# A filter phase rebuilt around pairs of units: four row groups, the sum of squares on VectorE, and queues held to program order

## The chip, the cores and the metric

The kernel runs on one core of a Trainium2 chip. The metric is the device time of one execution in microseconds (us). Engines are named as in the profile: PE is the matmul engine and PEld its weight loads, DVE is VectorE, ACT is ScalarE, POOL is GpSimd, SP is the queue that issues most transfers. All data is 32-bit floating point.

## The reference

Two layers are computed on an image batch of shape (4, 512, 512, 16). The first is a group norm, then a two-dimensional convolution whose filter is given in the frequency domain as a ratio of two polynomials, for each of 16 x 16 pairs of input channel i and output channel j:

```python
a = jnp.pad(denumerator, ((0,0),(0,0),(1,0),(1,0)), constant_values=1.0)
b = jnp.pad(numerators, ((0,0),(0,0),(0,0),(1,0),(1,0)), constant_values=0.0)
h_truncated = irfft2(rfft2(b, s=(l1, l2)) / rfft2(a, s=(l1, l2)), s=(l1, l2))
H_full = h0 + rfft2(h_truncated, s=(2*l1, 2*l2))[0]
y = irfft2(einsum('...hwi,ijhw->...hwj', rfft2(x, s=(2*l1, 2*l2)), H_full))[..., :l1, :l2, :]
```

The second layer is another group norm and a 3 x 3 convolution with normalised patches and an arccosine. Both layers are added to their inputs. The change concerns only the quotient of the two polynomials, evaluated at 512 x 512 frequencies for every pair (i, j).

## The kernel before

The program has four phases, one after another: the filter (`filter_phase`), the forward transform of the image, the convolution in frequency space, and the inverse transform with the second layer. The change lies wholly in the filter phase, the first 5840 us.

The filter phase is a software pipeline over 1024 units of work. A unit is one output channel j, one half h of the second frequency axis, one input channel i, and one half kp of the first frequency axis; the loop nests them in that order, kp innermost. A unit's tiles hold 128 partitions by 512 numbers: two blocks k of 128 first-axis frequencies, a real and an imaginary part c, and 128 second-axis frequencies.

Step v of the loop does, in program order:

- the next piece of `rest`, the odd frequencies of an output channel that is already done (`odd`): two matmuls of 512 columns into `pt` (L417), and the copy of the piece before it to `ot`, on DVE and ACT in turn (L423, L425), stored by SP. These begin once 72 units are done, so units 0 to 71 have none;
- every 64 steps `weights`, the polynomials of the next output channel;
- `polynomials` of unit v (L329): denominator (n = 0) and numerator (n = 1) are each evaluated by matmuls with a contraction of only 18 rows. The operands sit at partitions 32 (i mod 4) and 32 ((i mod 4) xor 1), so the two use two of the four 32-row groups of the matmul array. Each of the two PSUM tiles of a unit fills one bank; the pool `ps_ab` has four. ACT copies both to SBUF (`ab`, L335) and squares the denominator (`sq`, L337);
- every eight steps `quad` (L313, L315), which prepares the first-axis factors of four input channels: eight matmuls into four 32-column groups;
- `square` of unit v-1: POOL adds the two squares (`dn`, L341);
- `terms` of unit v-2: POOL makes real and imaginary part of the numerator from the products (L355, L356);
- `product` of unit v-1: DVE multiplies (`m`, L347) and takes the reciprocal (L348), POOL makes the two crossed products (`x`, L350 and L351);
- `quotient` of unit v-2: DVE scales both parts (`sp`, L361, two instructions) and, for h = 0, puts one column from `z` in (L364);
- `taps` of unit v-3: four matmuls with the whole array (`pg`, L372) and two ACT copies into the stage tile `st` (L377). After 32 units the two stage tiles go out to DRAM (L383). The stage pool has three tiles.

Beside all this, `image_stats` makes the group-norm statistics of the image (L544 on DVE, its loads issued by ACT).

Each engine runs its own queue in a fixed order. That order is made when the program is built: a scheduler places instructions greedily, by the dependencies and by a table of estimated durations, so an instruction that the program names late can be queued early. The statistics show it: the program spreads them over 1024 units, and in the trace they are done after 965 us.

Of the kernel before, what the change touches and what calls it, by code (L numbers as in the profile page):

```python
# [40 lines left out]
F32 = mybir.dt.float32  # L41
AF = mybir.ActivationFunctionType
# [4 lines left out]
P = 128  # L47
N = 512
B = 4
C = 16  # L50
# [150 lines left out]
def bc(ap, axis, shape):  # L201
    return ap.unsqueeze(axis).to_broadcast(shape)

# [21 lines left out]
def filter_phase(tc, cst, h0, num, den, g_d, beside):  # L229
    nc = tc.nc  # L230
    with ExitStack() as ctx:
# [3 lines left out]
        ew = ctx.enter_context(tc.tile_pool(name="f_ew", bufs=2))  # L235
# [3 lines left out]
        ps_ab = ctx.enter_context(tc.tile_pool(name="f_psab", bufs=4, space=PSUM))  # L239
# [4 lines left out]
        e2 = load_const(nc, cp, cst, "e2").rearrange("p (s h n) -> p s h n", s=2, h=2)  # L244
# [5 lines left out]
        def weights(j):  # L250

            sa = wt.tile([18, C, 32], F32, name="sa")
            sb = wt.tile([18, C, 32], F32, name="sb")
            nc.gpsimd.dma_start(out=sa.rearrange("p i n -> p (i n)"), in_=cst["apad"])
            nc.gpsimd.memset(sb, 0.0)
            for t, src in ((sa, den), (sb, num)):
                for c in range(2):
                    nc.gpsimd.dma_start(  # L260
                        out=t[9 * c + 1 : 9 * c + 9, :, 9 * c + 1 : 9 * c + 9],
                        in_=src[:, j].rearrange("i p q -> p i q"),
                    )
            ha = sm.tile([18, C, 18], F32, name="ha")
            nc.gpsimd.tensor_mul(ha, sa[:, :, 0:18], bc(h0b[:, j :: C], 2, [18, C, 18]))
            nc.gpsimd.tensor_add(sb[:, :, 0:18], sb[:, :, 0:18], ha)


            v = sm.tile([18, 2, 4, C], F32, name="v")
            ev = sm.tile([18, 2, 2, C], F32, name="ev")  # L270
            od = sm.tile([18, 2, 2, C], F32, name="od")
            for n, t in enumerate((sa, sb)):
                for c in range(2):
                    q = 9 * c
                    nc.vector.reduce_sum(ev[:, c, n, :], t[:, :, q : q + 9 : 2], axis=AX.X)
                    nc.vector.reduce_sum(od[:, c, n, :], t[:, :, q + 1 : q + 9 : 2], axis=AX.X)
            nc.vector.tensor_add(v[:, :, 0::2, :], ev, od)
            nc.vector.tensor_sub(v[:, :, 1::2, :], ev, od)
            pz = ps_t.tile([P, 4, 2, 4, C], F32, name="pz", tag="t")
            for k in range(4):  # L280
                nc.tensor.matmul(
                    pz[:, k].rearrange("p c v i -> p (c v i)"),
                    e1[:, k * P : (k + 1) * P],
                    v.rearrange("p c v i -> p (c v i)"),
                    start=True,
                    stop=True,
                )
            zs = sm.tile([P, 4, 2, 4, C], F32, name="zs")
            nc.scalar.copy(zs, pz)
            hz = sm.tile([P, 4, 2, 2, C], F32, name="hz")  # L290

            def half(c, v):
                return zs[:, :, c, v : v + 2, :].rearrange("p k v i -> p k (v i)")

            divide(nc, sm, half(0, 0), half(1, 0), half(0, 2), half(1, 2),
                   hz[:, :, 0].rearrange("p k v i -> p k (v i)"),
                   hz[:, :, 1].rearrange("p k v i -> p k (v i)"), [P, 4, 2 * C], "zd")
            z = wt.tile([P, 4, 2, C], F32, name="z")
            nc.vector.tensor_add(z[:, :, 0, :], hz[:, :, 0, 0, :], hz[:, :, 1, 1, :])
            nc.vector.tensor_sub(z[:, :, 1, :], hz[:, :, 1, 0, :], hz[:, :, 0, 1, :])  # L300
            return sa, sb, z

        def quad(sa, sb, iq):

            us = []
            for n, s in enumerate((sa, sb)):
                pu = ps_t.tile([P, N], F32, name=f"pu{n}", tag="t")  # L310
                for i in range(4):
                    at = 32 * (i ^ n)
                    nc.tensor.matmul(pu[at : at + 32], s[:, 4 * iq + i], e1, start=True, stop=True)  # L313
                u = wt.tile([P, N], F32, name=f"u{n}")
                nc.scalar.copy(u, pu)  # L315
                us.append(u)
            return us

        def polynomials(w):

            pp = [ps_ab.tile([P, 2, 2, P], F32, name=f"pab{n}", tag="ab") for n in range(2)]
            for k in range(2):
                k1 = (2 * w["kp"] + k) * P
                for n in range(2):
                    at = 32 * (w["i"] % 4 ^ n)
                    q = slice(at, at + 18)
                    nc.tensor.matmul(  # L329
                        pp[n][:, k].rearrange("p c n -> p (c n)"),  # L330
                        w["us"][n][q, k1 : k1 + P], e2[q, n, w["h"], :], start=True, stop=True,
                    )
            w["ab"] = [ew.tile([P, 2, 2, P], F32, name=f"ab{n}") for n in range(2)]
            for n in range(2):
                nc.scalar.copy(w["ab"][n], pp[n])  # L335
            w["sq"] = ew.tile([P, 2, 2, P], F32, name="sq")
            nc.scalar.activation(w["sq"], w["ab"][0], AF.Square)  # L337

        def square(w):
            w["dn"] = ew.tile([P, 2, P], F32, name="dn")  # L340
            nc.gpsimd.tensor_add(w["dn"], w["sq"][:, :, 0], w["sq"][:, :, 1])  # L341

        def product(w):

            a, b = w["ab"]
            w["m"] = ew.tile([P, 2, 2, P], F32, name="m")
            nc.vector.tensor_mul(w["m"], b, a)  # L347
            nc.vector.reciprocal(w["dn"], w["dn"])  # L348
            w["x"] = ew.tile([P, 2, 2, P], F32, name="x", bufs=1)
            nc.gpsimd.tensor_mul(w["x"][:, :, 0], b[:, :, 0], a[:, :, 1])  # L350
            nc.gpsimd.tensor_mul(w["x"][:, :, 1], b[:, :, 1], a[:, :, 0])  # L351

        def terms(w):
            m, x = w["m"], w["x"]
            nc.gpsimd.tensor_add(m[:, :, 0], m[:, :, 0], m[:, :, 1])  # L355
            nc.gpsimd.tensor_sub(m[:, :, 1], x[:, :, 1], x[:, :, 0])  # L356

        def quotient(w):
            sp = w["sp"] = ew.tile([P, 2, 2, P], F32, name="sp")
            for c in range(2):  # L360
                nc.vector.tensor_mul(sp[:, :, c], w["m"][:, :, c], w["dn"])  # L361
            if w["h"] == 0:
                kp = w["kp"]
                nc.vector.tensor_copy(sp[:, :, :, 0], w["z"][:, 2 * kp : 2 * kp + 2, :, w["i"]])  # L364
# [67 lines left out]
        def odds():  # L432

            for j in range(C):
                while done[0] < 64 * (j + 1) + 8:
                    yield
                yield from odd(j)

        work = [dict(j=j, h=h, i=i, kp=kp)
                for j in range(C) for h in range(2) for i in range(C) for kp in range(2)]  # L440
        done = [0]
        rest = odds()
        polys = {0: weights(0)}
        us = quad(*polys[0][:2], 0)
        for v in range(len(work) + 3):
            next(rest)
            if v % 64 == 32 and v < len(work) - 64:
                polys[v // 64 + 1] = weights(v // 64 + 1)
            if v < len(work):
                w = work[v]  # L450
                if v % 8 == 0 and v:
                    us = ahead
                w["us"], w["z"] = us, polys[w["j"]][2]
                polynomials(w)
                if v % 8 == 4 and v + 4 < len(work):
                    g = (v + 4) // 8
                    ahead = quad(*polys[g // 8][:2], g % 4)
            first, second, third = (work[v - k] if 0 <= v - k < len(work) else None for k in (1, 2, 3))
            if first:
                square(first)  # L460
            if second:
                terms(second)
            if first:
                product(first)
            if second:
                quotient(second)
            if third:
                if third["i"] == 0 and third["kp"] == 0:
                    st = [stp.tile([P, N, C], F32, name=f"st{a}", tag="st") for a in range(2)]
                third["st"] = st  # L470
                taps(third)
                done[0] += 1
                third.clear()
            if v % 2:
                next(beside, None)
# [915 lines left out]
```

## Time and profile before

| | |
|---|---|
| median of three runs | 18878.0 us (18847.71 to 18889.9) |
| profiled execution | 18884.85 us, of which the span of the core is 18883.1 us |
| filter units with statistics beside them | 0 to 1000 us (162 units) |
| the other filter units | 1000 to 5660 us (862 units) |
| odd frequencies of the last output channel | 5660 to 5840 us |
| forward transform | 5840 to about 6920 us |
| convolution and the last phase | 6920 us to the end |

Busy time in the two stages of the filter, in us:

| stretch | PE | DVE | ACT | POOL | granted PE clock |
|---|---|---|---|---|---|
| 0 to 1000 us | 820.74 | 864.04 | 457.75 | 674.54 | 0.85 |
| 1000 to 5660 us | 4462.42 | 3524.26 | 2642.29 | 3602.86 | 0.95 |

How to read it: a row of the groups names the line, the engine, the operation, the tile written and the tiles read, the shape and the number of instructions; after the bar stand the time in which at least one of them ran, the mean duration of one in ns, and the idle time of the engine just before them with what ended it. A 32-bit matmul appears as two records, so one call in the code is two instructions in a row of the profile. Matmuls overlap, so a record lasts longer than the step from one to the next.

### The profile page before, as it was taken

Reading aid. Unit: us, or ns where it says so; the run is one execution under the profiler, and the core shown is the slowest. Engines: PE = TensorE matmul, PEld = TensorE weight load, DVE = VectorE, ACT = ScalarE, POOL = GpSimd, SP = SyncE. Lnnn points to the kernel's source line nnn. Section 1 sums busy time; section 2 is a strip of 40 time slices with the busy share of each in tenths; the row PEclk is TensorE's granted clock in tenths of the full one; section 3 lists DMA queues with packets and bytes.
Section 4 is the critical chain, followed back from the end, with each engine's and each line's share of the span. In section 5 each row is a group of like instructions: output and inputs, shape, how many; then the busy total and the mean of one; then the engine's idle time right before and its main releaser. Section 6 shows DMA issues by size and latency. Waiting matters only on the chain. (4 is left out here: it accounts for less than half of the span.)

```text
span 18883.1 us, 533095 instructions
## 1 busy us (share of the span) xinstructions
PE 17055.0 (90%) x224908; PEld 12368.5 (66%) x224908; DVE 11526.1 (61%) x24155; ACT 9724.0 (51%) x17871; POOL 11616.7 (62%) x12701
## 2 busy tenths in 40 slices
PE   7899999999998998988888888888898988988898
PEld 5455555555554457777777777777777776877777
DVE  8877777777773335555555555555555555246887
ACT  4455555555552235555555555555555554005788
POOL 7577777777771126666666666666666666026776
PEclk8899999999999999999999999999999999998999
DMA  3755555455547668888888888888888888696432
GB/s 101 207 153 141 144 150 150 134 152 152 147 140 230 187 199 321 325 319 320 322 323 318 324 318 320 322 323 321 323 322 320 324 324 306 248 326 208 161 127 71
DMA packets 2918838, 4543.16 MB, mean 241 GB/s; under 512 B 117634, under 2 KB 2086492, under 8 KB 2809566
## 3 DMA queue, kind: packets, MB, share of 16 engines
q1 hardware_dynamic: 2686254, 3768.92, 59.1%
q0 software_dynamic: 174896, 605.89, 8.3%
q10 hardware_dynamic: 55296, 134.24, 2.1%
q8 instruction: 1773, 29.05, 0.6%
q14 instruction: 619, 5.07, 0.1%
HBM read 3031.24 MB, written 1477.31 MB: 239 GB/s over the span
## 5 line engine op out<-in xcount | busy, mean ns | idle before, releaser
L783 PE MATMUL pg<-c_dg,g 64*128 64x128 f32 x32832 | 2855.2, 291 | 347.3 <-ACT gh L683 193.2
L799 PE MATMUL pm<-xe,gh 128*32 128x64 f32 x131328 | 2394.6, 222 | 555.4 <-issue 297.3
L799 PEld LDWEIGHTS pm<-xe,gh 128*32 128x32 f32 x131328 | 2011.6, 111 | 1153.2 <-issue 962.1
L783 PEld LDWEIGHTS pg<-c_dg,g 64*128 64x128 f32 x32832 | 2292.4, 190 | 695.3 <-issue 257.2
L372 PE MATMUL pg<-c_dinv,sp 128*128 128x256 f32 x8192 | 2279.4, 426 | 296.0 <-ACT st L377 179.1
L828 DVE TENSOR_TENSOR z<-zq,pz 128x256 f32<-128x256 f32 x2052 | 861.8, 420 | 2665.9 <-ACT zq L827 2591.7
L348 DVE RECIPROCAL dn<-dn 128x256 f32<-128x256 f32 x1024 | 1790.8, 1749 | 774.7 <-POOL dn L341 774.6
L372 PEld LDWEIGHTS pg<-c_dinv,sp 128*128 128x128 f32 x8192 | 1611.1, 207 | 944.3 <-issue 213.0
L681 DVE COPY gh<-pg 128x512 f32<-128x512 f32 x2046 | 1410.0, 689 | 1247.7 <-PE pg L783 1244.0
L417 PE MATMUL pt<-ev_in,c_todd 128*128 128x512 f32 x4096 | 1974.9, 607 | 51.9 <-DMA ev_in<-g_d 27.3
L752 POOL TENSOR_TENSOR xu<-xe,c_late 128x256 f32<-128x256 f32 x2052 | 1393.7, 705 | 893.1 <-ACT xe L683 866.3
L683 ACT COPY yf<-pm 128x512 f32<-128x512 f32 x2046 | 1210.9, 592 | 935.8 <-PE pm L799 921.5
L335 ACT COPY ab<-pab 128x512 f32<-128x512 f32 x2048 | 1103.9, 591 | 1126.3 <-POOL m L355 323.9
L377 ACT COPY st<-pg 128x256 f32<-128x256 f32 x2048 | 1072.6, 622 | 1025.4 <-PE pg L372 629.3
L763 ACT COPY xe<-xl 64x1024 f32<-64x1024 f32 x513 | 538.6, 1050 | 1891.4 <-POOL xl L754 1891.4
L350 POOL TENSOR_TENSOR x<-ab,ab 128x256 f32<-128x256 f32 x1024 | 874.7, 854 | 922.9 <-ACT ab L335 896.4
L683 ACT COPY gh<-pg 128x512 f32<-128x512 f32 x2058 | 1201.1, 584 | 392.3 <-PE pg L783 383.0
L820 PE MATMUL pz<-c_ident,yf 128*128 128x128 f32 x8208 | 1373.7, 290 | 29.8 <-issue 28.0
L417 PEld LDWEIGHTS pt<-ev_in,c_todd 128*128 128x128 f32 x4096 | 807.5, 198 | 680.0 <-issue 518.2
L329 PEld LDWEIGHTS pab<-c_e,u 18*128 18x128 f32 x8192 | 719.0, 187 | 806.1 <-ACT st L377 458.3
L754 POOL TENSOR_TENSOR xl<-xl,xu 128x1024 f32<-128x1024 f32 x513 | 1209.7, 2358 | 40.2
L329 PE MATMUL pab<-c_e,u 18*128 18x256 f32 x8192 | 1186.5, 406 | 5.6 <-ACT ab L335 5.6
(205 smaller groups left out, 33831.8 us busy)
## 6 DMA issues: line engine op xcount, KB each, us to landing
xe<-xf_d SPq DMA_DIRECT2D x1026, 1536.0 KB, 10.7
g<-g_d SPq DMA_DIRECT2D x511, 1024.0 KB, 9.9
g_d<-st SPq DMA_DIRECT2D x64, 4096.0 KB, 34.5
ev_in<-g_d SPq DMA_DIRECT2D x1024, 256.0 KB, 4.8
g_d<-ot SPq DMA_DIRECT2D x1024, 256.0 KB, 2.8
xf_d<-xe POOLq DMA_DIRECT2D x513, 448.0 KB, 8.4
xf_d<-xl POOLq DMA_DIRECT2D x513, 448.0 KB, 5.4
x_d<-xo SPq DMA_DIRECT2D x128, 1024.0 KB, 5.1
```

The source lines that it names most:

```text
L329: nc.tensor.matmul(pp[n][:, k].rearrange("p c n -> p (c n)"), w["us"][n][q, k1 : k1 + P], e2[q, n, w["h"], :], start=True, stop=True,)
L335: nc.scalar.copy(w["ab"][n], pp[n])
L348: nc.vector.reciprocal(w["dn"], w["dn"])
L372: nc.tensor.matmul(pg[:, k].rearrange("p a x -> p (a x)"), w["sp"][:, k, c, :], dinv[:, 2 * kp + k, c, :], start=(c == 0), stop=(c == 1),)
L417: nc.tensor.matmul(pt, todd[:, c, kc, hh * P : hh * P + P], ev[:, kc, c], start=(kc == 0), stop=(kc == 1),)
L681: nc.vector.tensor_copy(dst, src)
L683: nc.scalar.copy(dst, src)
L752: nc.gpsimd.tensor_mul(u[:, :, h, c], xe[:, :, h, 1 - c], bc(late[:, 1 + c], 2, [P, F, 2]))
L754: nc.gpsimd.tensor_add(xl.rearrange("p f h c k -> p (f h c k)"), xl.rearrange("p f h c k -> p (f h c k)"), u.rearrange("p f h c k -> p (f ...
L783: nc.tensor.matmul(pg[c][:, j % 4], g[half, j], dg[half], start=True, stop=True)
L799: nc.tensor.matmul(pm[32 * q : 32 * q + 32, g % 8], gh[:, f].rearrange("p c j -> p (c j)"), xe[:, :, f].rearrange("p t h c k -> p t (h c k ...
L820: nc.tensor.transpose(pz[:, t % 4].rearrange("p v q x -> p (v q x)"), y[:, at].rearrange("p g x -> p (g x)"), ident)
```

## The change

Units are now made in pairs that share kp, h and j and whose input channels differ by two: (0,2), (1,3), (4,6), (5,7) and so on.

- `polynomials` takes a pair. It issues the eight matmuls of both units together, and since i mod 4 differs by two, the four polynomials lie in four different row groups. The pair takes all four PSUM tiles at once.
- The eviction becomes a function of its own, still per unit. The copies stay; the one square of 512 numbers is split in two of 256. The square of the real part goes to SBUF, the square of the imaginary part goes back into the denominator's PSUM tile, which therefore stays in use until it is read.
- `square` moves from POOL to DVE, reads one square from SBUF and one from PSUM, and now belongs to unit v, at the end of step v. `dn` gets three buffers.
- The two crossed products on POOL become one instruction of 512 numbers, the two scalings on DVE become one with `dn` repeated over the two parts.
- `quad` moves behind the units' work of the step.
- The class `InOrder` ties every unit instruction of PE, DVE, ACT and POOL to the one before it on its engine, so that the scheduler keeps these in program order. The work of `rest`, `weights`, `quad` and the statistics is not tied.

```diff
+class InOrder:
+    def __exit__(self, *_):
+        dep = mybir.DependencyInfo(mybir.DependencyClass.NoSync, mybir.DependencyReason.DATA)
+        for i in list(self.tc.nc.cur_bb.bb.instructions)[self.begin :]:
+            if i.engine in self.engines:
+                if i.engine in self.last:
+                    self.tc.add_manual_dep(i, self.last[i.engine], dep, reason="in order")
+                self.last[i.engine] = i.name
...
-        def polynomials(w):
-            pp = [ps_ab.tile([P, 2, 2, P], F32, name=f"pab{n}", tag="ab") for n in range(2)]
+        def polynomials(pair):
+            for w in pair:
+                w["pp"] = [ps_ab.tile([P, 2, 2, P], F32, name=f"pab{n}", tag="ab") for n in range(2)]
             for k in range(2):
-                k1 = (2 * w["kp"] + k) * P
-                for n in range(2):
...
+                for w in pair:
+                    k1 = (2 * w["kp"] + k) * P
+                    for n in range(2):
+                        at = 32 * (w["i"] % 4 ^ n)
+                        q = slice(at, at + 18)
+                        nc.tensor.matmul(
+                            w["pp"][n][:, k].rearrange("p c n -> p (c n)"),
+                            w["us"][n][q, k1 : k1 + P], e2[q, n, w["h"], :], start=True, stop=True,
+                        )
+
+        def evict(w):
             w["ab"] = [ew.tile([P, 2, 2, P], F32, name=f"ab{n}") for n in range(2)]
+            pp = w.pop("pp")
             for n in range(2):
                 nc.scalar.copy(w["ab"][n], pp[n])
-            w["sq"] = ew.tile([P, 2, 2, P], F32, name="sq")
-            nc.scalar.activation(w["sq"], w["ab"][0], AF.Square)
+            w["sq"], w["pa"] = ew.tile([P, 2, P], F32, name="sq"), pp[0]
+            nc.scalar.activation(w["sq"], w["ab"][0][:, :, 0], AF.Square)
+            nc.scalar.activation(pp[0][:, :, 1], w["ab"][0][:, :, 1], AF.Square)
 
         def square(w):
-            w["dn"] = ew.tile([P, 2, P], F32, name="dn")
-            nc.gpsimd.tensor_add(w["dn"], w["sq"][:, :, 0], w["sq"][:, :, 1])
+            w["dn"] = ew.tile([P, 2, P], F32, name="dn", bufs=3)
+            nc.vector.tensor_add(w["dn"], w["sq"], w.pop("pa")[:, :, 1])
...
-            nc.gpsimd.tensor_mul(w["x"][:, :, 0], b[:, :, 0], a[:, :, 1])
-            nc.gpsimd.tensor_mul(w["x"][:, :, 1], b[:, :, 1], a[:, :, 0])
+            nc.gpsimd.tensor_mul(w["x"], b, a[:, :, ::-1])
...
-            for c in range(2):
-                nc.vector.tensor_mul(sp[:, :, c], w["m"][:, :, c], w["dn"])
+            nc.vector.tensor_mul(sp, w["m"], bc(w["dn"], 2, [P, 2, 2, P]))
...
+                with order:
+                    if v % 2 == 0:
+                        pair = work[v : v + 2]
+                        pair[1]["us"] = us
+                        polynomials(pair)
+                    evict(w)
+            with order:
+                if second:
+                    terms(second)
+                if first:
+                    product(first)
+                if second:
+                    quotient(second)
+                if v < len(work):
+                    square(w)
+            if v % 8 == 4 and v + 4 < len(work):
+                g = (v + 4) // 8
+                ahead = quad(*polys[g // 8][:2], g % 4)
             if third:
...
-                taps(third)
+                with order:
+                    taps(third)
```

## The prediction

> **What bounds the kernel now.** I read the busy shares by stretch first, then the order of time inside one stretch, then the groups of that stretch and its waits.
>
> ```profile
> 1000.00:5660.00 4660.00, 4462.42 (x19043) 2652.02 (x19042) 3524.26 (x4514) 2642.29 (x4965) 3602.86 (x4478) 0.95 0.53 147
> ```
>
> The columns after the length are PE, PEld, DVE, ACT, POOL, clock, DMA share, GB/s. PE is busy 96%, every other engine 57 to 77%. The groups of this stretch count 862 products, so a unit takes 4660 / 862 = 5.41 us. A busy PE need not be at its peak, so I looked at the order of time:
>
> ```profile
> 3002.15 1.13 PE L329 MATMUL pab<-c_e,u 18*128 18x256 f32 x8
> 3003.21 1.99 PE L372 MATMUL pg<-c_dinv,sp 128*128 128x256 f32 x8
> 3005.05 1.88 PE L417 MATMUL pt<-ev_in,c_todd 128*128 128x512 f32 x4
> 3006.86 1.13 PE L329 MATMUL pab<-c_e,u 18*128 18x256 f32 x8
> 3007.92 1.06 PE L313 MATMUL pu<-c_e,sa 18*32 18x512 f32 x8
> ...
> 3009.77 1.56 PE L372 MATMUL pg<-c_dinv,sp 128*128 128x256 f32 x6
> ```
>
> From start to start, PE spends 1.06 us on the polynomials of a unit, 1.84 on its taps, 1.81 on a piece of odd frequencies, and 1.85 on a quad every eighth unit, with no gap. That is 1.06 + 1.84 + 1.81 + 1.85/8 = 4.94 us per unit. So PE itself sets 4.94 of the 5.41 us, and 0.47 are stalls. The largest stall that I can name:
>
> ```profile
> ACT st L377 <- DMA g_d<-st: 202.6, 27, 9.7
> ```
>
> It is 27 waits of 7.5 us (0.24 us a unit): a new stage tile waits until the third-last one has gone out. The rest is the start of each output channel and refilling after these waits.
>
> ```profile
> L348 DVE RECIPROCAL dn<-dn 128x256 f32<-128x256 f32 x862 | 1508.8, 1750 | 716.7 <-POOL dn L341 716.7
> L347 DVE TENSOR_TENSOR m<-ab,ab 128x512 f32<-128x512 f32 x862 | 751.6, 872 | 323.5 <-ACT ab L335 300.6 <-ACT st L377 0.5 <-issue 0.2
> L361 DVE TENSOR_TENSOR sp<-m,dn 128x256 f32<-128x256 f32 x1727 | 921.2, 574 | 0.0
> ```
>
> DVE waits 0.83 us a unit for POOL's sum of squares, and is second in line. The product takes 0.69 us undisturbed (its median over the phase), 0.87 here; the two scalings 2 x 0.35 undisturbed, 2 x 0.53 by their busy time. So 0.5 to 0.55 us per unit goes to DVE standing behind POOL.
>
> The first 1000 us are different: 162 units at 6.0 us (966 us from the first reciprocal), DVE busy 864 us because all 283 us of statistics (1024 x 276 ns) fall there, and no odd piece in the first 72 units. There DVE is the bound.
>
> **What the skill says.** The Trainium skill, "TensorE: Matmul & The Clock Gate", section "Measured speedup vs the span model", gives 3.07x for four row tiles of 32 rows by 512 columns. No run of before has four row groups. The trace has two: the 8 records of a unit start in pairs 6 ns apart, 216 ns from pair to pair, while taps make one record per 216 ns. And it has four column groups (L313), whose records start in fours within 20 ns and 429 ns apart. "TensorEngine Tiling (Array Packing)", section "Key Properties", says that changing the tiling mode drains the array; the trace agrees: 4 x 216 = 864 of the 1062 ns are streaming, about 104 are the first weight load and 94 the drain. "SBUF — State Buffer", section "Who interferes with whom", says that a DVE instruction with two SBUF inputs contends with a POOL instruction that reads SBUF, and that one with a single SBUF input does not. The trace agrees: in the second pair of lines below DVE issued 0.03 us after POOL and took 1.24 us, not 0.69.
>
> ```profile
> 3001.41 0.68 DVE L347 TENSOR_TENSOR m<-ab,ab 128x512 f32<-128x512 f32 x1
> 3001.43 1.24 POOL L341 TENSOR_TENSOR dn<-sq 128x256 f32<-128x256 f32 x1
> ...
> 3006.16 0.72 POOL L341 TENSOR_TENSOR dn<-sq 128x256 f32<-128x256 f32 x1
> 3006.19 1.24 DVE L347 TENSOR_TENSOR m<-ab,ab 128x512 f32<-128x512 f32 x1
> ```
>
> **The change part by part** (per unit, stretch after 1000 us).
>
> *Pairs in four row groups.* If four groups stream together, a pair is 16 records in four rounds: 104 + 4 x 216 + 94 = 1062 ns, or 0.53 per unit, saving 0.53. Upper bound of the cost: the groups go two by two, 8 rounds less one mode change, about 0.96 per unit, saving 0.1. A loss I exclude, since the same records in the same groups do not get longer by standing in a row. I take 0.53: the quad's records pass three waiting ones to reach a free group, so PE's queue can feed four. PE is then 0.53 + 1.84 + 1.81 + 0.23 = 4.41 us per unit.
>
> *Sum of squares.* POOL loses an add of 0.92 (mean here). DVE gains one of 256 numbers with one input in PSUM; the nearest row, of the convolution phase, is
>
> ```profile
> L828 DVE TENSOR_TENSOR z<-zq,pz 128x256 f32<-128x256 f32 x2052 | 861.8, 420 | 2665.9 <-ACT zq L827 2591.7 <-POOL z L838 71.7
> ```
>
> so +0.42 on DVE, and its 0.83 us of waiting for POOL is gone. The split square costs ACT one fixed part more: 512 numbers take 591 ns from PSUM (L335) and 256 take 377 (L827), so 0.84 ns a number and 0.16 fixed; +0.16 at most. ACT was busy 3.07 us per unit (2642/862), so 3.2 after: hidden below PE and DVE as long as it isn't waited for at once. It is waited for at the pair's start, see the rivals.
>
> *Merged products.* POOL's two products (0.85 + 0.96) become one of 512: 1.27 by the row of L836 (1273 ns). POOL falls from 4.18 to about 2.9. DVE's two scalings become one like the product, 0.69.
>
> *DVE's sum:* reciprocal 1.75 + product 0.69 + scaling 0.69 + add 0.42 + column 0.37/2 + odd copy 0.68/2 = 4.07. Behind POOL it stood 0.5; POOL reads SBUF for less time but is packed closer, so I keep 0.45 (ends: 0.2, and 0.97, which is a whole crossed product of 1.27 issued just ahead of each scaling, less the 0.3 us for which the reciprocal still covers it). With the 0.1 us per unit of weights work on DVE (7 us per 64 units), 4.6 us.
>
> *Program order and quad's place.* No instruction costs more. The queues of before already ran pab, pg, pt in the program's order (lines above). A quad is used four steps later, so its later place is covered by four units of work; without cover it would cost 1.85/8 = 0.23 per unit, what PE pays anyway. SP's issues stay where they were, one step after their copies; POOL's own transfers belong to `weights` and aren't tied. The new wait is that a pair needs all four PSUM tiles back. Behind it on PE stand taps of v-3 and v-2 and two odd pieces; for these ACT's stage copies and the odd copies wait.
>
> *Sum.* The bound moves from PE (4.94) to DVE (4.6), PE following at 4.41. Stalls that nothing here touches: stage waits 0.24 and some 0.1 of refilling. So 4.6 + 0.34 = 4.94 against 5.41: -0.47 x 862 = -405. The loop by which PE waits for DVE and DVE for PE will not be perfect: I give 0.08 back, +70. In the first 162 units DVE is the bound already: +0.42 for the add, -0.12 for one fixed part less in the scaling, about -0.15 of standing behind POOL: +0.15 x 162 = +25. The tail of odd frequencies (180 us) and all later phases stay. Total -310: from the profiled 18884.85 to 18575, which against the median of the runs (18878.0, 7 us lower) I give as 18570.
>
> **Rivals.**
> 1. *PE stays the bound and DVE hides fully.* 4.41 + 0.34 = 4.75: -0.66 x 862 = -570, first stage 0: 18,310. For it: POOL loses nearly a third of its work. Against: DVE's 4.07 leaves only 0.34 for standing behind POOL and weights.
> 2. *The four groups don't run together* (the change doesn't do what it says). PE stays at 4.84, gain 0.1 x 862 = 86, less the 25 of the first stage, less a pair's longer turn-round: 18,850. Against it: the quad's four-way starts.
> 3. *Slower: the PSUM turn-round becomes the bound.* Before, two units' tiles could be filled while two were read; now nothing is filled until DVE's add of the pair's second unit has read the last square. The loop: pair 1.06, ACT's four steps of the first unit 1.85, add 0.42, product 0.69, reciprocal 1.75, scaling 0.69 with 0.97 behind POOL, add 0.42, four hand-overs of 0.1, odd copy 0.68, half a column 0.18: 9.1 us per pair, just under the 9.2 that DVE needs anyway. It decides from (5.41 - 0.34) x 2 = 10.1 us on. If PE is in the middle of a 1.8 us piece whenever the add ends, up to 1.8 us come on top; with 1.5, the loop is 10.6: (5.3 + 0.34 - 5.41) x 862 = +200, first stage +25: 19,100. Against it: PE's other work between two pairs is 7.3 us, so in a steady loop PE has nothing left and stands at the pair when the add ends.
>
> **How the numbers follow.** Forecast as summed (18,400 to 18,720): 0.55. Rival 1: 0.10. Rival 2 and a partial gain with much lost in the loop (18,720 to 18,840): 0.13, and 0.05 within 0.2% (38 us, about what a measurement of this kernel can tell from no change). Rival 3: 0.17. Faster 0.78, same 0.05, slower 0.17. The range 18,400 to 18,860 leaves out rival 1's lower part (0.07) and most of rival 3 (0.13).
>
> **What would show it.** The polynomials' records starting in fours, a pair taking 1.06 to 1.3 us from start to start (2.0 under rival 2); 862 units of the later stretch at 4.9 to 5.1 us; reciprocals no longer waiting for POOL; DVE busier than PE (88 to 95%). PE waiting ahead of a pair's first matmul for DVE's add, by more than 1 us a pair, would show rival 3. The prediction is wrong if the scaling stands behind POOL for the whole 1 us in every unit, if the statistics are queued elsewhere, or if ACT's order makes the second unit's eviction late behind a stage copy that waits for its transfer.

## The result and the profile after

The changed kernel takes 18389.05 us (median of three runs, 18373.56 to 18397.62) against 18878.0 us: a ratio of 0.9745 with a 95% interval of 0.9731 to 0.9759, or 489 us less. It is faster, as forecast. The saving is larger than the 310 us of the sum, and the time lies 11 us below the low end of the range.

Where the time went, from the two profiled executions (spans 18883.1 and 18387.3 us, so -496):

| part | before, us | after, us | difference |
|---|---|---|---|
| first three output channels (192 units), from reciprocal to reciprocal | 1128.4 | 1076.4 | -52 |
| the other 831 units | 5.408 each | 4.906 each | -417 |
| whole filter phase, up to the first forward transform | 5847.8 | 5377.8 | -470 |
| forward transform | 1090.8 | 1088.3 | -2 |
| convolution | 9053.6 | 9033.7 | -20 |
| what follows | 2890.9 | 2887.5 | -3 |

The code of the convolution is unchanged. Over the profiles of all kernels of this study that phase took between 9012.8 and 9085.6 us, so its -20 is put down to nothing here.

The first view is that of busy times by stretch, for the stretch that answers to the one shown of before. The columns are again PE, PEld, DVE, ACT, POOL, clock, DMA share, GB/s.

```profile
1000.00:5160.00 4160.00, 3923.64 (x18703) 2382.49 (x18702) 3490.54 (x4541) 2572.07 (x5718) 2569.60 (x2706) 0.95 0.58 162
```

It holds 846 units, 4.92 us each. PE is busy 94%, DVE 84%, and POOL has fallen from 77% to 62%. The order of time on PE, for one pair:

```profile
4263.02 1.15 PE L352 MATMUL pab<-c_e,u 18*128 18x256 f32 x16
4264.10 1.99 PE L398 MATMUL pg<-c_dinv,sp 128*128 128x256 f32 x8
4265.93 1.88 PE L443 MATMUL pt<-ev_in,c_todd 128*128 128x512 f32 x4
4267.65 1.89 PE L398 MATMUL pg<-c_dinv,sp 128*128 128x256 f32 x8
4269.37 1.88 PE L443 MATMUL pt<-ev_in,c_todd 128*128 128x512 f32 x4
4271.18 1.15 PE L352 MATMUL pab<-c_e,u 18*128 18x256 f32 x16
```

Sixteen records of polynomials, a whole pair, take 1.08 us from start to start, where eight took 1.06. In the trace they start in fours, 6 to 8 ns apart within a four; the fours follow each other by 0.32 us once and by 0.216 us twice. The pair takes 8.16 us, 4.08 a unit. DVE and POOL of the same kernel, one step before (start, duration; a bracket is idle time and what ended it):

```profile
4259.03 1.74 DVE L376 RECIPROCAL dn<-dn 128x256 f32<-128x256 f32 x1
4259.18 0.73 POOL L382 TENSOR_TENSOR m<-m 128x256 f32<-128x256 f32 x1 [0.63 <-DVE m L375]
4259.99 0.72 POOL L383 TENSOR_TENSOR m<-x 128x256 f32<-128x256 f32 x1
4260.69 0.62 DVE L387 TENSOR_TENSOR sp<-m,dn 128x512 f32<-128x512 f32 x1
4260.79 1.66 POOL L378 TENSOR_TENSOR x<-ab,ab 128x512 f32<-128x512 f32 x1
4261.83 0.40 DVE L369 TENSOR_TENSOR dn<-sq,pab 128x256 f32<-128x256 f32 x1
4262.16 0.83 DVE L375 TENSOR_TENSOR m<-ab,ab 128x512 f32<-128x512 f32 x1
4262.91 1.74 DVE L376 RECIPROCAL dn<-dn 128x256 f32<-128x256 f32 x1
```

The scaling (L387) issues 0.1 us ahead of the crossed product (L378) and takes its undisturbed 0.62 us. It is the crossed product that is longer: 1.66, where its shortest is 1.256. The product (L375) then stands behind the crossed product. Two groups and three waits of the stretch (groups: busy, mean ns, idle before and its releaser; waits: us in total, times, longest):

```profile
L376 DVE RECIPROCAL dn<-dn 128x256 f32<-128x256 f32 x846 | 1471.5, 1739 | 0.0
L369 DVE TENSOR_TENSOR dn<-sq,pab 128x256 f32<-128x256 f32 x845 | 347.5, 411 | 470.5 <-ACT pab L365 468.7
```

```profile
ACT st L403 <- DMA g_d<-st: 275.7, 26, 13.1
PEld pab L352 <- DVE dn L369: 82.6, 53, 3.6
PE pab L352 <- DVE dn L369: 59.7, 39, 3.2
```

The reciprocals wait for nobody. The add costs 0.41 us and waits 0.55 us a unit for ACT's second square. PE and its weight loads wait for DVE's add at most 142 us in 423 pairs. And the wait for the stage tile has grown: 26 waits of 10.6 us, where there were 27 of 7.5.

In the steps from one reciprocal to the next, after the first three channels, every 32 units (one h) hold one or two long steps, those that wait for the stage tile. Before: 13.2 and 7.0 us, the other thirty 5.10 on average. After: 18.1 us, the other thirty-one 4.48. So 5.10 + 0.31 became 4.48 + 0.43 us a unit, the second term being what the long steps have over the others, shared out over 32.

### The profile page after: what moved, and what is told of

It reads as the page before. It is cut to its first block, busy times and chain, and to the rows that moved or that the text cites. A ratio compares the mean times of both kernels' runs of the same rounds, so it can differ in the third digit from the quotient of the medians.

```text
span 18387.3 us, 530668 instructions
## 1 busy us (share of the span) xinstructions
PE 16516.6 (90%) x224908; PEld 12124.1 (66%) x224908; DVE 11547.2 (63%) x24155; ACT 9712.8 (53%) x18895; POOL 10465.0 (57%) x10653
## 5 line engine op out<-in xcount | busy, mean ns | idle before, releaser
L398 PE MATMUL pg<-c_dinv,sp 128*128 128x256 f32 x8192 | 2179.2, 414 | 223.9 <-ACT st L403 209.9
L378 POOL TENSOR_TENSOR x<-ab,ab 128x512 f32<-128x512 f32 x1024 | 1505.1, 1470 | 1039.3 <-ACT ab L361 993.9
L382 POOL TENSOR_TENSOR m<-m 128x256 f32<-128x256 f32 x1024 | 753.9, 736 | 885.8 <-DVE m L375 884.7
L1269 PE MATMUL pc<-l_band,xn 128*128 128x160 f32 (+2 forms) x6144 | 1079.4, 334 | 51.0 <-DVE e_o L1324 50.8
```

What stands on the lines that cost most here:

```text
L378: nc.gpsimd.tensor_mul(w["x"], b, a[:, :, ::-1])
L398: nc.tensor.matmul(pg[:, k].rearrange("p a x -> p (a x)"), w["sp"][:, k, c, :], dinv[:, 2 * kp + k, c, :], start=(c == 0), stop=(c == 1),)
```

## Experiments

The theory going in was that of the prediction: PE set the pace, packing a pair relieves it, moved and merged work makes room on DVE and POOL. The rival: the work moved off POOL carries the gain and the packing little. As the runs came in, a third was formed: two bounds lay side by side, and both had to go.

Times are medians. Ratios are to the kernel before on the same chip, with 95% intervals. "Half pair" is half of the time in which two units pass, from the first reciprocal of a pair to the first of the next, as the median over all halves h = 0 and over all halves h = 1 after the first three channels; "unit" is the mean over those 831 units, long steps included.

| kernel | us | ratio | half pair h=0 / h=1, us | unit, us |
|---|---|---|---|---|
| after | 18389.05 | 0.9745 (0.9731 to 0.9759) | 4.28 / 4.08 | 4.906 |
| e1, pairs in two row groups | 18681.72 | 0.9900 (0.9886 to 0.9915) | 4.51 / 4.51 | 5.210 |
| e2, no pairs | 18779.18 | 0.9950 (0.9934 to 0.9966) | 4.70 / 4.70 | 5.346 |
| e8, before with pairs alone | 18927.63 | 1.0024 (1.0014 to 1.0035) | 4.83 / 4.83 | 5.425 |
| e6, sum on POOL | 18596.21 | 0.9852 (0.9837 to 0.9867) | 4.56 / 4.49 | 5.115 |
| e7, products not merged | 18511.21 | 0.9807 (0.9792 to 0.9821) | 4.38 / 4.14 | 5.008 |
| e5, queues not tied | 18489.74 | 0.9793 (0.9778 to 0.9807) | 4.74 / 4.46 | 4.975 |
| e3, no column copy | 18291.11 | 0.9693 (0.9677 to 0.9708) | 4.08 / 4.08 | 4.830 |
| e4, stage tile split | 18108.85 | 0.9602 (0.9586 to 0.9618) | 4.28 / 4.08 | 4.651 |
| e9, e4 and column copy on POOL | 18105.5 | 0.9576 (0.9562 to 0.9590) | 4.08 / 4.08 | 4.617 |
| e11, e9 and stage stores from ACT | 18480.5 | 0.9767 (0.9749 to 0.9784) | 4.08 / 4.08 | 4.997 |

Two units are taken together because, where PE sets the pace, the steps of a pair are unequal: with h = 1 the changed kernel has medians of 3.89 and 4.27 us in turn, 8.16 together, and 8.16 is PE's own time for a pair.

### Is it the packing of the array?

**e1: the same pairs, but of neighbouring input channels**, whose four polynomials fall on two row groups instead of four.

```diff
-                for i in (i2 // 4 * 4 + i2 // 2 % 2, i2 // 4 * 4 + i2 // 2 % 2 + 2)]
+                for i in (i2, i2 + 1)]
```

> The changed kernel with other partners: the pairs are the input channels (0,1), (2,3) and so on, whose four polynomials share two row groups instead of using four. The pair, the four PSUM tiles taken at once, the queues' order and all else stay. Theory A (PE sets much of the pace, and the four groups are what relieves it): a pair takes 104 + 8 x 216 + 94 = 1.93 us instead of 1.08, PE needs 0.96 + 1.83 + 1.77 = 4.56 us a unit without a quad, against steps of 4.28 us (h = 0) and 4.08 (h = 1) now: +0.28 and +0.48, so +250 to +400 us on 18389. Theory B (the gain comes from VectorE no longer waiting for GpSimd, PE was not really full): 0 to +60 us.

It is 293 us slower than the changed kernel, as theory A had it. PE's order of time in e1:

```profile
3019.84 2.00 PE L352 MATMUL pab<-c_e,u 18*128 18x256 f32 x16
3021.76 1.99 PE L398 MATMUL pg<-c_dinv,sp 128*128 128x256 f32 x8
...
3028.85 1.35 PE L352 MATMUL pab<-c_e,u 18*128 18x256 f32 x10
```

The pair now takes 1.92 us and the next begins 9.01 us later, against 1.08 and 8.16. Everything else in the program is the same, so four groups streaming together are worth 0.42 us a unit on PE, and 0.30 us of that arrive in the unit (5.210 against 4.906). With h = 1 all of it does (4.51 against 4.08), with h = 0 only 0.23, since there something else had already held 4.28.

**e2: no pairs**, polynomials unit by unit, all other parts of the change kept.

```diff
-                    if v % 2 == 0:
-                        pair = work[v : v + 2]
-                        pair[1]["us"] = us
-                        polynomials(pair)
+                    polynomials([w])
```

> The changed kernel with the polynomials of one unit at a time, as before: two row groups, two PSUM tiles at once, so that the next unit's tiles can be filled while the last are read. All else of the change stays. Theory A: PE is back at 1.06 + 1.83 + 1.81 = 4.71 us a unit without a quad, +0.43 and +0.63 us a unit against now: +350 to +500 us, so the kernel is within 150 us of the one before. Theory B: 0 to +60 us, or a little faster than the changed kernel, since the tiles are double again.

It is 390 us slower than the changed kernel, again as theory A had it. PE's order of time in e2:

```profile
3009.05 1.13 PE L352 MATMUL pab<-c_e,u 18*128 18x256 f32 x8
3010.11 1.99 PE L398 MATMUL pg<-c_dinv,sp 128*128 128x256 f32 x8
3011.94 1.88 PE L443 MATMUL pt<-ev_in,c_todd 128*128 128x512 f32 x4
3013.75 1.13 PE L352 MATMUL pab<-c_e,u 18*128 18x256 f32 x8
```

Nothing lies between them: the typical half pair of 4.70 is PE's own 1.06 + 1.83 + 1.81. With the pairs taken out, PE is the bound, as the prediction said of the kernel before. But this also says that all of the change without the pairs is worth only 0.5%.

**e8: the kernel before with the pairs and nothing else.**

```diff
-        def polynomials(w):
+        def polynomials(pair):
...
-                for j in range(C) for h in range(2) for i in range(C) for kp in range(2)]
+                for j in range(C) for h in range(2) for i2 in range(0, C, 2) for kp in range(2)
+                for i in (i2 // 4 * 4 + i2 // 2 % 2, i2 // 4 * 4 + i2 // 2 % 2 + 2)]
...
-                polynomials(w)
+                if v % 2 == 0:
+                    pair = work[v : v + 2]
+                    pair[1]["us"] = us
+                    polynomials(pair)
+                evict(w)
```

> The kernel before with the pairs in four row groups alone (the order of the units and the eight matmuls together); sum of squares on GpSimd, two products, two scalings, no ties. Theory A: PE needs 4.08 us, VectorE 4.3 with its waits for GpSimd, GpSimd 4.2 busy: 4.3 to 4.7 us a step and the same stage waits, -130 to -400 us against 18878. Theory B: PE's relief alone gives nothing while VectorE waits for GpSimd's add: 0 to -60 us.

This one the first theory missed, and the other's 0 to -60 us did not come either. The pair runs in four groups here too, and PE needs some 0.5 us a unit less, yet the kernel is 52 us slower than before. Of these, 43 lie in the first three output channels (1171.7 against 1128.4 us); why is open. After them its half pairs are 4.83 us for both h. So something else holds 4.83, just below the 4.94 us that PE had needed.

### What the second bound is

**e12: the kernel before, with all odd pieces put off to the end of the phase.** PE then has only 1.06 + 1.84 + 0.23 = 3.13 us of work in a unit; DVE and ACT lose the odd copies. Only the steps of this kernel mean anything, not its total, since the odd pieces then run alone at the end.

```diff
-                while done[0] < 64 * (j + 1) + 8:
+                while done[0] < 64 * C + 8:
```

> The kernel before with all odd pieces put after the last unit. PE then needs 1.06 + 1.83 = 2.9 us a unit. If PE alone set the pace before (the prediction's reading): the steps fall to VectorE's own sum, 3.7 plus 0.5 behind GpSimd, 4.2 us or less. If VectorE and GpSimd hold each other in a loop just below PE's time (4.83 us in the run with pairs alone): the steps stay at 4.8 us.

The half pairs are 4.82 us for both h. One step, DVE and POOL only, in order of time:

```profile
2999.25 1.75 DVE L348 RECIPROCAL dn<-dn 128x256 f32<-128x256 f32 x1 [0.61 <-POOL dn L341]
...
2999.97 0.72 POOL L356 TENSOR_TENSOR m<-x 128x256 f32<-128x256 f32 x1
...
3000.78 0.72 POOL L350 TENSOR_TENSOR x<-ab,ab 128x256 f32<-128x256 f32 x1
3000.92 1.73 DVE L361 TENSOR_TENSOR sp<-m,dn 128x256 f32<-128x256 f32 x2
3001.46 0.90 POOL L351 TENSOR_TENSOR x<-ab,ab 128x256 f32<-128x256 f32 x1
...
3002.75 0.69 DVE L347 TENSOR_TENSOR m<-ab,ab 128x512 f32<-128x512 f32 x1
3002.79 1.24 POOL L341 TENSOR_TENSOR dn<-sq 128x256 f32<-128x256 f32 x1 [0.43 <-DVE sp L361]
...
3003.99 0.72 POOL L355 TENSOR_TENSOR m<-m 128x256 f32<-128x256 f32 x1
3004.06 1.75 DVE L348 RECIPROCAL dn<-dn 128x256 f32<-128x256 f32 x1 [0.62 <-POOL dn L341]
```

Neither engine is busy all the time, and yet neither can go faster. The two scalings take 1.73 us instead of 0.7, because they stand behind POOL's products; POOL's add takes 1.24 instead of 0.71, because it stands behind DVE's product; and the reciprocal waits for that add. The Trainium skill, "SBUF — State Buffer", section "Who interferes with whom", says that a DVE instruction with two SBUF inputs contends with a POOL instruction that reads SBUF, and that whichever comes first holds the shared access for its whole length. These lines agree. If so, POOL's instructions and DVE's products and scalings form one queue, whose lengths add up. With the shortest duration of each in the trace of before: add 0.713, crossed products 0.714 and 0.717, terms 0.712 and 0.718, scalings 2 x 0.348, product 0.621. That is 4.89 us; measured are 4.82. The sum was made after the run, and it counts whole durations, though a part of each may not need the access.

A rival would be a loop of waits with room in it: `dn` has two buffers here, and POOL's add waits 0.43 us for DVE's scaling to be done with one. But there is next to no room. In e12, the time of a step in which none of these instructions is under way is 0.19 us for h = 0 and 0.26 for h = 1, and its longest piece is 0.08 and 0.10 (medians over the 831 steps).

**e10: the changed kernel with the same edit.**

> The changed kernel with all odd pieces put after the last unit (nothing left out), so that PE needs only 0.54 + 1.83 = 2.4 us a unit beside them and the pace of VectorE and GpSimd shows by itself. The total is longer, the steps of the units count. By the prediction's sum of durations (4.07 - 0.34 odd copy - 0.18 column + 0.45 behind GpSimd) a step of h = 1 takes 4.0 us. If neighbours in VectorE's queue overlap by 0.08 us each and only the product is held up: 1.66 + 0.55 + 0.33 + 0.61 + 0.2 = 3.3 to 3.6 us; 0.4 to 0.55 more for h = 0.

Both numbers were missed. For h = 1 the half pair is 3.88 us, not the sum's 4.0 nor the 3.3 to 3.6 of the other view. The queue, by the shortest durations in the trace of after (crossed product 1.256, terms 0.712 and 0.713, scaling 0.616, product 0.672), gives 3.97. For h = 0 it is 4.28 with and without odd pieces. One such step:

```profile
4548.90 1.74 DVE L376 RECIPROCAL dn<-dn 128x256 f32<-128x256 f32 x1
...
4550.57 0.62 DVE L387 TENSOR_TENSOR sp<-m,dn 128x512 f32<-128x512 f32 x1
4550.68 1.63 POOL L378 TENSOR_TENSOR x<-ab,ab 128x512 f32<-128x512 f32 x1
...
4551.22 1.11 DVE L390 COPY sp<-z 128x4 f32<-128x4 f32 x1
...
4552.24 0.41 DVE L369 TENSOR_TENSOR dn<-sq,pab 128x256 f32<-128x256 f32 x1
...
4552.57 0.68 DVE L375 TENSOR_TENSOR m<-ab,ab 128x512 f32<-128x512 f32 x1
...
4553.18 1.74 DVE L376 RECIPROCAL dn<-dn 128x256 f32<-128x256 f32 x1
```

The column copy of four numbers a partition, whose shortest is 0.10 us, takes 1.11: it ends 0.02 us after POOL's crossed product (4552.31). The add behind it, which for h = 1 runs while the crossed product does, now comes after it, and costs the step its full 0.33 us from start to start. That is most of the 0.40 between 3.88 and 4.28. The same section of the skill names copies among the instructions that can hold both accesses, and so contend with POOL; this line agrees. The prediction had read from that section that an instruction with a single SBUF input does not contend; the section excepts such instructions as these copies, and this one, with its single input in SBUF, stands behind POOL.

**e3: the changed kernel without the column copy**, whose values are left out.

```diff
-            if w["h"] == 0:
-                kp = w["kp"]
-                nc.vector.tensor_copy(sp[:, :, :, 0], w["z"][:, 2 * kp : 2 * kp + 2, :, w["i"]])
```

> The changed kernel without the copy of the column from z on VectorE in the units of h = 0 (that part of the filter is left wrong). Theory A' (VectorE, packed without a gap, sets the pace in the halves h = 0, PE in the halves h = 1): the steps of h = 0 fall from 4.28 to 4.08 us, -0.20 x 430, and 0.55 in some 80 early units: -90 to -140 us. If PE sets the pace throughout: 0 to -20 us. If VectorE does throughout, the halves h = 1 would not be faster than the others, which they are already.

98 us less, within what was expected. The half pair of h = 0 falls from 4.28 to 4.08, which is PE's own, and that of h = 1 stays there. 0.20 us for each of the 512 copies would be 102 us.

**e6: the sum of squares back on POOL**, from one square of 512 numbers, the rest as after.

```diff
-            nc.vector.tensor_add(w["dn"], w["sq"], w.pop("pa")[:, :, 1])
+            nc.gpsimd.tensor_add(w["dn"], w["sq"][:, :, 0], w["sq"][:, :, 1])
```

> The changed kernel with the sum of squares back on GpSimd (one square of 512 numbers on ScalarE, all in SBUF); pairs, merged products and ties stay. Theory A (pairs carry most of the gain): VectorE loses 0.33 us of queue and waits again for GpSimd, whose loop (terms 1.5, product 1.65, add 0.75 us behind the start of the reciprocal, 0.2 of hand-over) is about as long as PE's unit: +0 to +150 us. Theory B (the gain is VectorE no longer waiting for GpSimd): +300 us or more, most of the 490 gone.

207 us more, between the two expectations. The queue comes nearer than either did: crossed product 1.260, terms 0.712 and 0.719, add 0.713, scaling 0.619, product 0.620 make 4.64; measured are 4.56 (h = 0) and 4.49 (h = 1). Four lines of e6 show the add behind DVE's product again, and that product behind the crossed one:

```profile
3000.31 1.86 POOL L377 TENSOR_TENSOR x<-ab,ab 128x512 f32<-128x512 f32 x1
...
3001.16 1.56 DVE L374 TENSOR_TENSOR m<-ab,ab 128x512 f32<-128x512 f32 x1
3002.14 1.17 POOL L368 TENSOR_TENSOR dn<-sq 128x256 f32<-128x256 f32 x1
...
3003.34 1.75 DVE L375 RECIPROCAL dn<-dn 128x256 f32<-128x256 f32 x1
```

**e7: products and scalings not merged**, the rest as after.

```diff
-            nc.gpsimd.tensor_mul(w["x"], b, a[:, :, ::-1])
+            nc.gpsimd.tensor_mul(w["x"][:, :, 0], b[:, :, 0], a[:, :, 1])
+            nc.gpsimd.tensor_mul(w["x"][:, :, 1], b[:, :, 1], a[:, :, 0])
...
-            nc.vector.tensor_mul(sp, w["m"], bc(w["dn"], 2, [P, 2, 2, P]))
+            for c in range(2):
+                nc.vector.tensor_mul(sp[:, :, c], w["m"][:, :, c], w["dn"])
```

> The changed kernel with two instructions each for the crossed products and for the scaling, as before. VectorE's two scalings step by about 0.28 us each, as long as the merged one's 0.55, and GpSimd's two products take 0.2 us more: +0 to +60 us. If standing behind each other on the shared port is what the merging saves (0.4 us a unit): +150 us or more.

122 us more, again between the two. The queue: four POOL instructions 2.86, scalings 0.70, product 0.67, together 4.23, against 4.14 for h = 1 and, with the column, 4.38 for h = 0. For h = 1 the sum of the queue is thus 0.07 to 0.15 us too high in all four kernels (e12, e10, e6, e7).

### The ties

**e5: nothing tied to program order.**

```diff
-        order = InOrder(tc, nc.tensor, nc.vector, nc.scalar, nc.gpsimd)
+        order = ExitStack()
```

> The changed kernel without the ties: the scheduler orders every queue by its own estimates. PE's and GpSimd's queues stay nearly the same, in VectorE's the product of a unit often moves ahead of the add of the unit after it, in ScalarE's the evictions move ahead of the stage copies. If the ties carry part of the gain: +60 us or more against 18389. If pairs and VectorE's shorter queue carry it: within 60 us of 18389.

101 us more than the changed kernel, so the ties carry part of the gain. The steps are more uneven: 83 times in the 831 units, one of about 2.1 us is followed by a long one (7.5 us in the median), because two reciprocals stand together in DVE's queue and the products of the later unit come afterwards. That this costs the 101 us is read from the trace alone.

### The stage tile

**e4: a stage tile of half the size for each kp**, six buffers instead of three, hence the same memory, each stored as soon as its own 16 units are in.

```diff
-        stp = ctx.enter_context(tc.tile_pool(name="f_stage", bufs=3))
+        stp = ctx.enter_context(tc.tile_pool(name="f_stage", bufs=6))
...
-            if i == C - 1 and kp == 1:
+            if i == C - 1:
...
-                    nc.sync.dma_start(
+                    for q in range(2):
+                        nc.sync.dma_start(
...
-                    st = [stp.tile([P, N, C], F32, name=f"st{a}", tag="st") for a in range(2)]
+                    sts[third["kp"]] = [stp.tile([P, N // 2, C], F32, name=f"st{a}", tag="st") for a in range(2)]
```

> The changed kernel with each stage tile cut in two by the half kp of the first frequency axis (six half tiles instead of three, the same memory). The halves with kp = 0 are complete two units before those with kp = 1 and are stored then; the same bytes go to the same places, in transfers of a quarter. Theory A'' (the wait for a stage tile is the largest stall that is left, and all that stands behind it is lost): the step at each change of h, 18 us now against 4.3, and the slow one after it fall to about 6; 31 changes x 10 to 14 us: -300 to -430 us. Rival: the wait covers transfers that something else waits for next (the odd pieces' loads and stores share SP's queue), so the time only moves: 0 to -100 us.

280 us less than the changed kernel, a little short of what was expected, and 4% less than the kernel before. No wait of ACT for a stage tile is left in its stretch from 1000 to 4800 us, the longest step of the 32, 18.1 us, is now 9.2, and PE is busy 97% (3684.88 of 3800 us). The largest wait for a store is now that of the odd copies:

```profile
DVE ot L451 <- DMA g_d<-ot: 80.9, 26, 7.0
```

So the smaller stage tiles bring 280 us on top of the 489 of the whole change.

**e9: e4 with the column copy on POOL** instead of DVE.

```diff
-                nc.vector.tensor_copy(sp[:, :, :, 0], w["z"][:, 2 * kp : 2 * kp + 2, :, w["i"]])
+                nc.gpsimd.tensor_copy(sp[:, :, :, 0], w["z"][:, 2 * kp : 2 * kp + 2, :, w["i"]])
```

> The changed kernel with the stage tiles cut in two (as in the run before that one, 18109 us) and the copy of the column from z moved from VectorE to GpSimd, behind the crossed product in its queue. If VectorE sets the pace in the halves h = 0 and GpSimd has room (2570 of 4160 us busy): -60 to -100 us against the split stage alone, 18,010 to 18,050. If GpSimd, standing at the column until the scaling is done, makes the terms of the next unit late: no gain, or slower than 18109.

The half pair of h = 0 falls from 4.28 to 4.08 and the filter phase from 5096.5 to 5042.4 us, but the median is only 3 us below that of e4. The two ran on different chips, and the kernel before took 18907.74 us on that of e9 and 18867.82 on that of e4. By the ratios, e9 is 0.26% or some 49 us faster than e4, a little less than expected; the two intervals just overlap. In the profile of e9 the convolution takes 9077.8 us where it took 9012.8 in that of e4, with the same code; why is open. e4 and e9 are the fastest kernels of the study.

**e11: e9 with the stage stores issued by ACT** instead of SP.

```diff
-                        nc.sync.dma_start(
+                        nc.scalar.dma_start(
```

> The run before with the stage stores issued by ScalarE instead of SP, so that the stores of the odd pieces no longer stand behind them (36 waits, 135 us in all, up to 20 us, with the split stage). If that queue is what is waited for: -50 to -130 us against the run before. If it is the transfers' own time on the shared transfer engines: within 30 us of the run before.

375 us more than e9; neither expectation held. ACT's waits in e11:

```profile
ACT ab L361 <- DMA g_d<-ot: 315.8, 25, 15.3
ACT ab L361 <- DMA g_d<-st: 226.3, 26, 13.4
```

Evictions of PSUM are now held, 51 times, 10.6 us each; in e9 no wait of ACT for a transfer is listed. An eviction needs nothing of a store. ACT's order of time shows what it stands behind (ACTq is ACT's queue while it issues):

```profile
1253.96 15.07 ACTq L410 DMA_DIRECT2D g_d<-st  x4
1269.13 1.07 ACT L361 COPY ab<-pab 128x512 f32<-128x512 f32 x2 [14.76 <-DMA g_d<-ot]
```

The issues of four stores of 1 MB take 15 us of ACT's queue here (8.2 to 15.6 in this stretch, 10.3 in the median), and the eviction comes next in it. The long steps at a change of h are 14.5 and 14.1 us (h = 0), and 12.2 and 11.6 (h = 1).

## Why the prediction was right and wrong

**Right.** *Pairs in four row groups*: 1.08 us for a pair from start to start, summed as 1.062; PE's 4.08 us a unit and 0.23 for the quad are the 4.31 beside the predicted 4.41. e1 shows that it is the four groups that do it. *Sum of squares*: +0.41 us on DVE, summed as +0.42, and the reciprocals' wait for POOL is gone. *Split square on ACT*: 0.43 and 0.39 us, ACT busy 62%; PE isn't held by it. *Rival 3*: PE waits for DVE's add, but at most 142 us in 423 pairs, 0.34 us a pair, and not more than 1 us. *Rival 2* falls with e1. *Rival 1*, that PE stays the bound, is half true: with h = 1 the 4.08 is PE's, and DVE and POOL could do 3.88 (e10).

**Half right: "PE itself sets 4.94 of the 5.41 us".** PE does, but not alone. The queue of POOL and DVE on the shared access held 4.82 to 4.83 (e8, e12). The prediction had all its parts: a product of 1.24 instead of 0.69, 0.5 us of scaling behind POOL, 0.83 us of waiting for POOL. It booked them as surcharges on DVE, "second in line", instead of adding up the queue. That is why pairs alone gain nothing (e8), all the rest alone gains 0.5% (e2), and both together 2.6%. The forecast of the whole change came out on the right side because the change lowers both: PE from 4.94 to 4.31, the queue from 4.82 to 3.88 (h = 1) and 4.28 (h = 0).

**Wrong: "DVE's sum", 4.6 us.** This is the step that failed most. It adds up DVE's instructions as if each lengthened the unit. The odd copy, 0.34 us a unit in the sum, does not: for h = 0 the half pair is 4.28 with odd pieces and 4.28 without (e10). In the trace of after the copy runs while POOL's crossed product does, in time in which DVE would stand at the column anyway:

```profile
3395.38 1.64 POOL L378 TENSOR_TENSOR x<-ab,ab 128x512 f32<-128x512 f32 x1
3395.82 0.67 DVE L449 COPY ot<-pt 128x512 f32<-128x512 f32 x1
3396.41 0.64 DVE L390 COPY sp<-z 128x4 f32<-128x4 f32 x1
```

Without the odd copy and the weights the sum's own terms give 4.37 for h = 0 and 4.00 for h = 1, and e10 measured 4.28 and 3.88. So "I keep 0.45" for standing behind POOL was about right in size, but not in place: the scaling comes first (0.62 us, undisturbed) and the crossed product of POOL waits, then DVE's product waits for that one. DVE's instructions also follow each other some 0.08 us before the end of the one ahead (a reciprocal of 1.74 is 1.66 from start to start). So the bound moved to DVE and POOL for h = 0 alone, at 4.28 instead of 4.6, and stayed with PE for h = 1. The sign "DVE busier than PE (88 to 95%)" did not come: DVE 84%, PE 94%.

**Wrong: "Stalls that nothing here touches: stage waits 0.24".** The stage waits rose from 7.5 to 10.6 us each. That the units come sooner while a store still needs its time (at least 17.9 us before, 17.2 after, of 4 MB) is the likely reason; no run tests it. e4, in which these waits are gone, is 280 us faster.

**Wrong: the first stage, +25 us.** It was -52 over 192 units. The two scalings of the first 64 units, where the statistics crowd DVE, kept it busy for 1.31 us a unit, the merged one does for 0.64: -0.67, where the sum had -0.12 and -0.15. That this is the reason is read from the trace; no run tests it. The last of the statistics starts later, at 1071.5 instead of 964.6 us. Two small slips change nothing: the 283 us of statistics are summed durations, of which 225.5 are busy time, and the terms given for POOL make 2.72 us a unit, not 2.9 (3.04 were measured).

**The sum of the miss.** In spans: -496 against -310, a difference of -186. Of it -77 is the first stage (-52 against +25), -82 the other units (-417 against -405 + 70), and -26 lies after the filter and isn't explained. The -82 hides two larger errors. Without the long steps, a unit was expected to come down to 4.6 + 0.1 + 0.08 = 4.78 and is at 4.48; the stage waits were expected at 0.24 and cost 0.43 by their long steps. The first error alone would be about -250 us over 831 units, and the second takes about +160 back. So it is luck that the time lies as near to the range as it does. (The prediction counted 162 and 862 units where this account has 192 and 831.)

## What to carry to other kernels

When DVE's two-input instructions and POOL's instructions stand behind each other in the trace, add their undisturbed durations as if they were one engine, and put that sum beside PE's: here 4.89 beside 4.94, so that relieving either alone was worth next to nothing. What reads PSUM, as the odd copy and DVE's add do here, can fit in beside them. A wait for a buffer that is being stored need not stay the same when the work ahead of it gets faster (here 7.5 became 10.6 us); look whether the buffer can go out in smaller parts (here 280 us for the same memory). And a small copy on an engine that shares an access can cost what it stands behind, not what it moves.

## What was not expected of the hardware

- A copy of four numbers a partition has a median of 1.11 us in e10 (shortest 0.10), standing behind POOL.
- A square of 256 numbers takes ACT 0.39 us when it is written to PSUM and 0.43 when it is written to SBUF (means of 845), both read from SBUF. The one written to PSUM always comes second, so the place in the queue is not ruled out as the reason.
- Stores issued from ACT's queue cost 375 us of a kernel in which the same stores, issued by SP, held no instruction of ACT.
